# A linear-attention and expert block on Trainium2: keys with tokens on partitions made from the features' operands, behind the features' quad

## The chip, the cores and the metric

The kernel runs on one core of a Trainium2 chip. The core has a matrix engine (TensorE, PE in the profile, with its weight loads listed apart as PEld), a vector engine (VectorE, DVE), an activation engine (ScalarE, ACT), a general engine (GpSimd, POOL) and a queue that here only issues DMA transfers (SyncE, SP). Each works through its own list of instructions, and they are tied together by semaphores. Matrix products land in PSUM, which has eight banks of 128 partitions by 512 float32 values; everything else lives in SBUF. The metric is the time of one execution on the device in microseconds (us), lower is better, taken as the median of several runs.

## The reference

Input x is 2 x 2048 x 256, float32. Two residual steps follow each other, each scaled and shifted by a small modulation (`ca, sa, ga` and `cb, sb, gb`, computed from `L0_c` and `L0_wmod`):

```python
def _phi(x, omega):                       # 16 heads of 16; omega is 16 x 128
    proj = jnp.einsum('bhtd,dm->bhtm', x, omega)
    norm_sq_half = 0.5 * jnp.sum(x * x, axis=-1, keepdims=True)
    return jnp.exp(proj - norm_sq_half) / math.sqrt(m)
...
kv = phi_k[..., :, None] * v[..., None, :]
S = jnp.cumsum(kv, axis=2)                # running sum over tokens
Z = jnp.cumsum(phi_k, axis=2)
num = jnp.einsum('bhtm,bhtmd->bhtd', phi_q, S)
den = jnp.einsum('bhtm,bhtm->bht', phi_q, Z)[..., None] + EPS
y = num / den                             # then @ W_proj + b_proj
```

The second step is a feed-forward net (256 to 1024 to 256, relu) with four experts that differ by low-rank additions of rank 4; a router picks two of the four for each token and weighs their outputs:

```python
base = jnp.einsum('bsd,fd->bsf', x, Wi)
lora = jnp.einsum('bser,efr->bsef', jnp.einsum('bsd,erd->bser', x, A), B)
h = jax.nn.relu(base[:, :, None, :] + lora)
out = jnp.einsum('bse,bsed->bsd', w, jnp.einsum('bsef,df->bsed', h, Wo))
```

## The kernel before

**Tiling.** The 4096 tokens are eight blocks of 512 (`N = 8`; blocks 0 to 3 are one sequence, 4 to 7 the other). Within a block the 16 heads are four groups of four, and the 512 tokens are four chunks of 128. The main loop (L1091) takes a block in eight rounds, `k = 0..7`: round k finishes two chunks of group k // 2, and prepares the next two, which the code calls `following`. A round is written (block, round) below.

**Attention in a round.** The running sum is handled chunk by chunk. `features` (L470) makes the exponents of 128 features for four heads, 512 tokens each: four products of 32 rows that lie side by side in the array, "the features' quad", each filling one bank; `exponentials` (L482) turns them into `phi` on ACT. Features are on partitions and tokens along the row there. `scores` (L545) multiplies key features by query features within a chunk into the two fixed banks `pa[0]` and `pa[1]`; `mask` (L559) multiplies that by a triangle on DVE; `outputs` (L609) adds the masked scores times v and the earlier state times the query features into a bank `py`; `keep_outputs` (L632) copies it out on ACT. The state needs the keys the other way round, with tokens on partitions: `increments` (L569) multiplies such keys by v into the second half of the same bank `py`, `keep_increments` (L583) copies that out on DVE as `ds`, and in the next round `states` (L592) transposes and adds it to the state S.

**Two ways to have keys with tokens on partitions.** `keys` (L494) transposes `phi` chunk by chunk on PE into a bank `pk`, four transposes a chunk, and `keep_keys` (L539) copies the bank on ACT; `turn` (L1098) does this for both chunks of `following`. `key_rows` (L515) instead multiplies the features' operand f by omega with the roles exchanged, 32 rows and 128 columns a head, and `keep_key_rows` (L527) applies the exponential on ACT. Before, this second way is used only where a unit of the feed-forward net has four open banks with unused second halves.

**The rest of the work.** While attention of block i runs, the other work is laid between its parts by `run_full` (L946), whose table `steps` says for each round what PE does before scores: for the next block (`a = i + 1`) the transposes `channels1`, the products `query_key` and `values`; for the block before (`p = i - 1`) `project`, `channels2`, `low_rank`, `weigh`; and for `p` or `q = i - 2` the feed-forward net. Its first half goes in units: `hidden` (L826) opens four banks, `first` (L842) and `second` (L852) add the two experts' low-rank parts and apply relu, on ACT and on DVE (`r`, L864); `finish` (L867) is its second half. `unit_keys` (L970) is a unit whose banks also take key rows. In blocks 2 to 6 rounds 0, 1, 2 and 7 hold a unit, and their keys come from it; rounds 3 to 6 hold none. Blocks 0 and 1 have no unit but the one in (1, 7), and it takes no keys.

**Banks.** PSUM is shared by three kinds of tile: `pa[0]` and `pa[1]`, one bank each; "mm" tiles (`mm_tile`, L84), a ring of four banks; and "side" tiles (`side_tile`, L87), a ring of two. A ring hands out its banks in turn, and a new tile waits until its bank has been read. The features' quad takes all four "mm" banks, `py` takes a "side" bank.

**Order.** The order of instructions on each engine is the order in which the code writes them; `keep_written_order` (L22) fixes it. After `run_full` a round writes what `whole` (L1054) lists for it (layer norm statistics and norms on DVE, gates), the router in round 5, then scores, increments and outputs, the two copies, the quad for a later group with its exponentials, the masks, what `amid` (L1035) lists (the division, and the SP transfers that bring the operands f of the next block from DRAM, `reload`, L444), and `behind` (L1070: loads, the choice of experts, the bias).

Of the kernel before, what the change touches and what calls it, by code (L numbers as in the profile page):

```python
# [14 lines left out]
P = 128  # L15
NH = 16
DH = 16
# [15 lines left out]
def kernel(  # L33
# [53 lines left out]
    def side_tile(name):  # L87
        return psum.tile([P, TB], FP, tag="side", name=name, bufs=2)
# [291 lines left out]
    def query_key(i, n):  # L380
        s = st[i]
        pq = side_tile(f"pq{i}_{n}")
# [67 lines left out]
    def values(i, t):  # L450
# [4 lines left out]
        pv = side_tile(f"pv{i}_{t}")  # L455
# [59 lines left out]
    def key_rows(chunks, banks):  # L515


        for j, bank in enumerate(banks):
            rs = slice(2 * DH * j, 2 * DH * (j + 1))
            for i, g, t in chunks:  # L520
                c0 = TH + (t % 2) * P
                nc.tensor.matmul(  # L522
                    bank[:, c0 : c0 + P], st[i]["feat"][1, g][rs, t * P : (t + 1) * P], om[rs, :],
                    start=False, stop=True, skip_group_check=True, tile_position=(2 * DH * j, 0),
                )

    def keep_key_rows(chunks, banks):  # L527
        kts = [key_tile(*chunk) for chunk in chunks]
        i, g, t = chunks[0]
        n = len(chunks)  # L530
        for j, bank in enumerate(banks):
            nc.scalar.activation(
                pair[i, g, t // 2][:, 0:n, j, :],
                bank[:, TH : TH + n * P].rearrange("p (n m) -> p n m", m=M), AF.Exp, bias=lnm,
            )
        for chunk, kt in zip(chunks, kts):
            turned[chunk] = kt

    def keep_keys(i, g, t):  # L539
        if (i, g, t) in turned:  # L540
# [311 lines left out]
    def second(i, u, chunks=()):  # L852

        s = st[i]
        banks, f0, ts, whole_banks = s["unit"].pop(u)
        if chunks:
            key_rows(chunks, whole_banks)
        low_step(s, 1, banks, f0, ts)
        if chunks:
            keep_key_rows(chunks, whole_banks)  # L860
        for j, ph in enumerate(banks):
            g = s["g"][f0 + j][:, ts]
            r = work.tile([P, TH], FP, tag="r", name=f"r{i}_{u}{j}", bufs=RG)
            nc.vector.scalar_tensor_tensor(r, ph, 0.0, s["rho"][:, ts], ALU.max, ALU.mult)  # L864
            nc.gpsimd.tensor_add(g, g, r)  # L865
# [77 lines left out]

    PAIRS = NG * NT // 2

    def run_full(i, k, turn, state, following):  # L946


        a, p, q = i + 1, i - 1, i - 2

        def qk(n):
            query_key(a, n)

        def v(*ts):
            for t in ts:
                values(a, t)

        def ff(t, *part):
            finish(q, t, *part)
            if t == 3 and (not part or part[-1] == NF):  # L960
                store(q)

# [7 lines left out]
        def unit_keys(of, which, *between):  # L970
# [3 lines left out]
                do(*args)  # L974
            second(of, which, [chunk for chunk in following if carried(chunk[0], chunk[2])])

        def projection():
            project(p, 0, NT)

        mm, side, s = (turn, mm_tile), (turn, side_tile), (state,)  # L980
        split = (turn, side_tile, (0,)), (turn, mm_tile, (1,))
        if i == 0:
            steps = (
                (s, (values, 0, 2), (values, 0, 3), mm),
                (s, *split),
                (s, (channels1, a, side_tile, mm_tile), mm, (qk, 2)),
                (s, (qk, 0), mm),
                (s, (qk, 3), (gate, 0, 0), mm),
                (s, (v, 0), (gate, 1, 0), mm),
                (s, (v, 1, 2), (columns, 1), mm),  # L990
                (s, (qk, 1), (v, 3), mm),
            )
        elif i == 1:
            steps = (
                (s, (channels1, a, side_tile, mm_tile), mm, (qk, 2), (v, 0), (gate, 0, 1)),
                (s, (qk, 0), (v, 1), mm),
                (s, mm, (projection,)),
                (s, (qk, 3), mm),
                (s, *split, (channels2, p), (gate, 1, 1)),
                (s, *split),  # L1000
                (s, *split),
                (s, (v, 2), (low_rank, p), (qk, 1), (weigh, p), side, (hidden, p, 0),
                 (unit, p, 0, (v, 3))),
            )
        elif a < N:
            steps = (
                ((channels1, a), (hidden, q, 1), s, (v, 0), (unit_keys, q, 1, (qk, 2))),
                (s, (v, 1), (hidden, q, 2), (unit_keys, q, 2, (qk, 0))),
                (s, (v, 2), (hidden, q, 3), (unit_keys, q, 3, (qk, 3))),
                (s, (projection,), mm),  # L1010
                (s, (ff, 0), (channels2, p), mm),
                (s, (ff, 1), mm),
                (s, (ff, 2), mm, (low_rank, p)),
                ((weigh, p, side_tile), (state, mm_tile), (ff, 3, mm_tile, 0, NF), (v, 3),
                 (hidden, p, 0), (unit_keys, p, 0, (qk, 1))),
            )
        else:
            half = side_tile, 0, RG
            rest = None, RG, NF
            steps = (  # L1020
                (s, (turn, side_tile, (0,)), (hidden, q, 1),
                 (unit, q, 1, (turn, side_tile, (1,)))),
                (s, (ff, 0, *half), (hidden, q, 2), (unit, q, 2, (ff, 0, *rest), side)),
                (s, (ff, 1, *half), (hidden, q, 3), (unit, q, 3, (ff, 1, *rest), side)),
                (s, (projection,), mm),
                (s, *split, (channels2, p)),
                (s, *split),
                ((ff, 2), s, mm),
                ((low_rank, p), (ff, 3, side_tile, 0, 3), (weigh, p), s, (ff, 3, None, 3, 6),
                 (hidden, p, 0), (unit, p, 0, (ff, 3, None, 6, NF))),  # L1030
            )
        for do, *args in steps[k]:
            do(*args)

    def amid(i, k):  # L1035
# [8 lines left out]
                norm2(p)  # L1044
        if a < N:
            late = int(i == 0)
            n = {2 + late: 2, 3 + late: 0, 4 + late: 3, 7: 1}.get(k)
            if n is not None:
                reload(a, n, 0)
                reload(a, n, 1)  # L1050
# [6 lines left out]
        (0, 6): ((norm1_stats, 2),),  # L1057
        (0, 7): ((norm1, 2),),
        (1, 1): ((gate_wo, 0, 0, NF),),
        (1, 3): ((norm2, 0), (norm1_half, 3, 0)),  # L1060
        (1, 4): ((norm1_half, 3, 1),),
        (1, 5): ((gate_wo, 1, 0, NF),),
        (1, 6): ((choose, 0),),
        (1, 7): ((norm1, 3),),
    }
    for i in range(2, N - 2):
        whole[i, 4] = ((norm1_stats, i + 2),)
        whole[i, 6] = ((norm1, i + 2),)

    def behind(i, k):  # L1070
# [20 lines left out]
    for i in range(N):  # L1091
        for k in range(PAIRS):
# [146 lines left out]
```

## Time and profile before

| | us |
|---|---|
| median of 3 runs | 758.35 (757.79 to 758.4) |
| the profiled execution | 756.79 |
| its span, first to last instruction | 755.0 |
| PE busy / weight loads busy | 744.8 / 552.1 |
| DVE / ACT / POOL busy | 407.0 / 329.6 / 148.3 |
| granted TensorE clock | 1.00 |

The profile is of one execution. A row of the groups names the line, the engine and the operation, then the tile written and the tiles read ("out<-in"), the shape, the number of instructions, then the busy time in us, the mean length of one in ns, and after the second bar the time for which the engine stood idle just before them, with what ended it. Matrix products of float32 appear twice each, as do their weight loads. The view in order of time lists the start in us, the length, the engine, the line and the tiles, with equal neighbours merged; a bracket at the end gives the idle time just before and what released it. Products overlap in the array, so lengths of PE rows overlap too; the distance from one group's start to the next one's is what a group takes.

### The profile page before, as it was taken

To read this page: it belongs to the slowest core of one execution; us is meant where nothing else is said; L and a number is where in the kernel's file an instruction comes from. 1 tells how busy PE (TensorE), PEld (TensorE's weight loads), DVE (VectorE), ACT (ScalarE), POOL (GpSimd) and SP (SyncE) were. 2 spreads that over 40 slices of the span, in tenths; PEclk is the share of its full clock that TensorE was granted. 3 is DMA by queue.
4 is the path that set the end of the run, shared out by engine and by line. 5 is a ranking of instruction groups with operands and counts; after the bars stand their busy time and mean duration, and the time that the engine had idled before them with its cause. 6 is when DMAs were issued, how large, how long until landed. Compare 5 with 4: busy or idle time off the path is not lost.

```text
span 755.0 us, 24542 instructions
## 1 busy us (share of the span) xinstructions
PE 744.8 (99%) x10720; PEld 552.1 (73%) x10720; DVE 407.0 (54%) x1133; ACT 329.6 (44%) x742; POOL 148.3 (20%) x192
## 2 busy tenths in 40 slices
PE   9999999999999999999999999999999999999998
PEld 6667776666787767776787677877688777777776
DVE  5667667564663547534656456645364424654612
ACT  1665546535544444435544455435454343521010
POOL 3000322222210322011220122103130112005122
PEclk9999999999999999999999999999999999999999
DMA  4369443123301433023420342204240130002000
GB/s 134 111 195 298 146 143 100 44 82 120 114 29 32 129 112 114 17 72 119 124 72 33 111 125 82 67 29 130 73 127 16 50 110 17 16 34 83 1 29 28
DMA packets 44234, 65.46 MB, mean 87 GB/s; under 512 B 6752, under 2 KB 20256, under 8 KB 44128
## 3 DMA queue, kind: packets, MB, share of 16 engines
q1 hardware_dynamic: 42240, 62.33, 26.1%
q8 instruction: 84, 1.38, 0.8%
q10 hardware_dynamic: 1888, 1.58, 0.7%
q14 instruction: 22, 0.18, 0.1%
HBM read 35.32 MB, written 28.57 MB: 85 GB/s over the span
## 4 chain that ended last, share of the span: by engine, by line
PE 93%; DVE 4%; ACT 1%; issue 1%; DMA 0%; POOL 0%; DVEq 0%
PE ph L836 13%; PE pf L874 12%; PE pa L552 9%; PE pp L476 9%; PE pq L384 7%; PE ph L821 4%; PE pk L500 4%; PE pv L457 4%; PE py L621 4%; PE py L576 4%; PE py L627 3%; PE po L682 3%; PE pt L597 3%; PE pf L896 2%; PE ph L522 2%; PE pta L331 1%
## 5 line engine op out<-in xcount | busy, mean ns | idle before, releaser
L865 POOL TENSOR_TENSOR g<-g,r 128x256 f32<-128x256 f32 x128 | 90.6, 741 | 416.3 <-DVE r L864 416.3
L487 ACT ACTIVATE phi<-pp,lnm 128x512 f32<-128x512 f32 x256 | 155.2, 689 | 9.7 <-PE pp L476 3.6
L874 PE MATMUL pf<-wo_g,g 128*128 128x256 f32 x448 | 103.6, 382 | 0.4 <-ACT phi L487 0.2
L836 PE MATMUL ph<-h,wi_sb 128*128 128x256 f32 x448 | 101.9, 380 | 0.1
L836 PEld LDWEIGHTS ph<-h,wi_sb 128*128 128x128 f32 x448 | 84.3, 190 | 12.5 <-DVE r L864 0.5
L874 PEld LDWEIGHTS pf<-wo_g,g 128*128 128x128 f32 x448 | 82.6, 190 | 13.7 <-issue 2.2
L552 PEld LDWEIGHTS pa<-phi,phi 128*32 128x32 f32 x4096 | 77.5, 110 | 14.8 <-issue 13.3
L552 PE MATMUL pa<-phi,phi 128*32 128x128 f32 (+3 forms) x4096 | 85.4, 235 | 0.1
L850 ACT ACTIVATE g<-ph 128x256 f32<-128x256 f32 x112 | 33.9, 389 | 115.1 <-PE ph L821 115.1
L635 ACT COPY y<-py 128x128 f32<-128x128 f32 x128 | 27.8, 269 | 125.2 <-DVE ds L588 123.4
L561 DVE TENSOR_TENSOR am<-pa,causal 128x512 f32<-128x512 f32 x128 | 81.8, 681 | 0.0
L391 DVE TENSOR_SCALAR qs<-pq,bqk 128x512 f32<-128x512 f32 x30 | 22.5, 751 | 99.3 <-PE pq L384 94.6
L476 PE MATMUL pp<-f,om 32*128 32x512 f32 x512 | 73.6, 640 | 0.0
L542 ACT COPY kt<-pk 128x512 f32<-128x512 f32 x82 | 44.5, 594 | 54.8 <-PE pk L500 54.7
L864 DVE SCALAR_TENSOR_TENSOR r<-ph,rho 128x256 f32<-128x256 f32 x112 | 41.7, 422 | 45.6 <-PE ph L821 23.2
L384 PE MATMUL pq<-hT,w_sb 128*128 128x512 f32 x120 | 58.5, 612 | 0.0
L588 DVE COPY ds<-py 128x256 f32<-128x256 f32 (+1 forms) x63 | 25.7, 407 | 52.6 <-PE py L627 47.0
L621 PE MATMUL py<-am,v 128*32 128x128 f32 x1024 | 51.4, 273 | 0.0
L627 PE MATMUL py<-phi,S 128*32 128x128 f32 x960 | 50.1, 273 | 0.0
L597 PEld LDWEIGHTS pt<-ident,ds 128*128 128x128 f32 x120 | 12.8, 140 | 44.6 <-DVE ds L588 38.7
L500 PE MATMUL pk<-ident,phi 128*128 128x128 f32 x328 | 44.9, 275 | 0.5 <-ACT phi L487 0.4
L500 PEld LDWEIGHTS pk<-ident,phi 128*128 128x128 f32 x328 | 37.7, 141 | 7.1 <-ACT phi L487 3.0
(159 smaller groups left out, 968.2 us busy)
## 6 DMA issues: line engine op xcount, KB each, us to landing
f<-qd SPq DMA_DIRECT2D x60, 256.0 KB
qd<-qs SPq DMA_DIRECT2D x58, 256.0 KB
ydr<-y SPq DMA_DIRECT2D x32, 256.0 KB
num<-ydr SPq DMA_DIRECT2D x16, 256.0 KB
inv<-rdr SPq DMA_DIRECT2D x16, 256.0 KB
xt<-in_x_dram SPq DMA_DIRECT2D x7, 512.0 KB
out_dram<-xt SPq DMA_DIRECT2D x7, 512.0 KB
wo_g<-in_woT_dram SPq DMA_DIRECT2D x2, 1024.0 KB
```

Source lines behind the costliest of these rows:

```text
L384: nc.tensor.matmul(pq, w_sb[:, k, n * P : (n + 1) * P], s["hT"][:, k, :], start=(k == 0), stop=(k == KC - 1),)
L476: nc.tensor.matmul(pp, om[rs, :], f[rs, :], start=True, stop=True, tile_position=(2 * DH * j, 0))
L487: nc.scalar.activation(ph, pps[j], AF.Exp, bias=lnm)
L500: nc.tensor.transpose(pk[:, j * P : (j + 1) * P], phi[i, g, 1, j][:, t * P : (t + 1) * P], ident)
L542: nc.scalar.copy(kt.rearrange("p h m -> p (h m)"), turned[i, g, t])
L552: nc.tensor.matmul(pa[t % 2][c * CG : (c + 1) * CG, j * P + q0 : j * P + q1], phi[i, g, 1, j][:, t0 + c * CG : t0 + (c + 1) * CG], phi[i, ...
L561: nc.vector.tensor_mul(am, pa[t % 2][:].rearrange("p (h q) -> p h q", h=HG), causal[t % 2][:].unsqueeze(1).to_broadcast([P, HG, P]),)
L621: nc.tensor.matmul(py[rows[j], :], v[:, t, g * HG + j, :], am[:, j, :], start=True, stop=state is None,)
L627: nc.tensor.matmul(py[rows[j], :], state[:, rows[j]], phi[i, g, 0, j][:, tok], start=False, stop=True,)
L836: nc.tensor.matmul(ph, wi_sb[:, k, f * P : (f + 1) * P], s["h2"][:, k, ts], start=(k == 0), stop=False, skip_group_check=True,)
L865: nc.gpsimd.tensor_add(g, g, r)
L874: nc.tensor.matmul(po, s["g"][f][:, t * P : (t + 1) * P], wo_g[i // NBLK][:, f, :], start=(f == 0), stop=(f == NF - 1), skip_group_check=True,
```

## The change

The rounds without a unit get their keys from `key_rows` too. A new function `keys_behind_features` takes four banks, `pa[0]`, `pa[1]` and two "side" tiles, writes the key rows of `following` there at the very start of the round, which is straight behind the quad that ended the round before, and has ACT apply the exponential to them. `key_rows` and `keep_key_rows` get the first column and the start flag as arguments. Which round does what is told by two new functions:

```diff
+    def keys_behind_features(i, g, t):
+        banks = pa + [side_tile(f"pk{i}_{g}{t}{n}") for n in range(2)]
+        chunks = [(i, g, u) for u in (t, t + 1) if carried(i, u)]
+        key_rows(chunks, banks, 0, True)
+        keep_key_rows(chunks, banks, 0)
...
+    def keys_first(i, k):
+        return i == 0 or (k < 7 if i == 1 else 3 <= k <= 6 if i < N - 1 else 3 <= k <= 5)
+
+    def keys_in_unit(i, k):
+        return k == 7 if i == 1 else 1 < i and (k < 3 or k == 7) and (i < N - 1 or k in (1, 2))
...
+        tile = mm_tile if keys_first(i, k) else side_tile
...
+        if keys_first(i, k):
+            keys_behind_features(*following[0])
         for do, *args in steps[k]:
             do(*args)
```

In those rounds the state step, `query_key`, `values`, `project`, `finish` and block 0's and 1's `channels1` take "mm" tiles in place of "side" tiles, and `mm`, `side` and `split`, the turns, leave the table of steps. Two rows of it, as examples:

```diff
-                (s, (projection,), mm),
-                (s, (ff, 0), (channels2, p), mm),
+                (s, (projection,)),
+                (s, (ff, 0), (channels2, p)),
```

Rounds (1, 7), (7, 1) and (7, 2) change from a unit and turns to `unit_keys`; (1, 7) also gets a new order of its steps (`low_rank` first, the values `v` and `query_key` later), and values 1 move from (1, 1) to (1, 2). Turns stay in (7, 0) and (7, 6) and for the first two chunks of all.

The order at the end of a round changes in every round, and outputs come ahead of increments wherever keys come from `key_rows`:

```diff
-            late_keys = 1 < i < N - 1 and k in (0, 1, 2, 7)
+            late_keys = keys_first(i, k) or keys_in_unit(i, k)
             if late_keys:
                 outputs(i, g, (t, t + 1), bank)
             added = increments(following, bank)
             if not late_keys:
                 outputs(i, g, (t, t + 1), bank)
+            for chunk in following:
+                mask(*chunk)
             keep_increments(*added)
             keep_outputs(i, g, (t, t + 1), bank)
 
             gi, gg = divmod(n // NT + 1 + k % 2, NG)
             if gi < N:
                 exponentials(*features(gi, gg, k % 2))
-            for chunk in following:
-                mask(*chunk)
```

Some smaller steps move to other rounds:

```diff
-            n = {2 + late: 2, 3 + late: 0, 4 + late: 3, 7: 1}.get(k)
+            n = {2 + late: 2, 3 + late: 0, 6: 3, 7: 1}.get(k)
...
-        (1, 3): ((norm2, 0), (norm1_half, 3, 0)),
-        (1, 4): ((norm1_half, 3, 1),),
-        (1, 5): ((gate_wo, 1, 0, NF),),
+        (1, 2): ((norm1_half, 3, 0),),
+        (1, 3): ((norm2, 0),),
+        (1, 5): ((norm1_half, 3, 1), (gate_wo, 1, 0, NF)),
...
     for i in range(2, N - 2):
-        whole[i, 4] = ((norm1_stats, i + 2),)
         whole[i, 6] = ((norm1, i + 2),)
```

The statistics taken out of round 4 are now a step of round 2 (`next_stats`, between `values` and `hidden`); the loads of the key operands f of groups 2 and 3 go from round 4 (5 in block 0) to round 6.

More of the change, by code (lines that the diff above doesn't have):

```diff
@@ L378, in channels1, with query_key @@
         s["feat"], s["qd"] = {}, {}
-    def query_key(i, n):
+    def query_key(i, n, tile=side_tile):
         s = st[i]
-        pq = side_tile(f"pq{i}_{n}")
+        pq = tile(f"pq{i}_{n}")
         for k in range(KC):
@@ L448, in reload, with values @@
         st[i]["feat"][side, g] = f
-    def values(i, t):
+    def values(i, t, tile=side_tile):
         s = st[i]
@@ L454, in values @@
             nc.gpsimd.memset(s["v"][:, :, :, DH:HW], 1.0)
-        pv = side_tile(f"pv{i}_{t}")
+        pv = tile(f"pv{i}_{t}")
         for k in range(KC):
@@ L513, in key_tile, with key_rows @@
         return pair[n][:, t % 2]
-    def key_rows(chunks, banks):
+    def key_rows(chunks, banks, c0, start):
         for j, bank in enumerate(banks):
@@ L520, in key_rows, with keep_key_rows @@
             for i, g, t in chunks:
-                c0 = TH + (t % 2) * P
+                c = c0 + (t % 2) * P
                 nc.tensor.matmul(
-                    bank[:, c0 : c0 + P], st[i]["feat"][1, g][rs, t * P : (t + 1) * P], om[rs, :],
-                    start=False, stop=True, skip_group_check=True, tile_position=(2 * DH * j, 0),
+                    bank[:, c : c + P], st[i]["feat"][1, g][rs, t * P : (t + 1) * P], om[rs, :],
+                    start=start, stop=True, skip_group_check=True, tile_position=(2 * DH * j, 0),
                 )
-    def keep_key_rows(chunks, banks):
+    def keep_key_rows(chunks, banks, c0):
         kts = [key_tile(*chunk) for chunk in chunks]
@@ L533, in keep_key_rows @@
                 pair[i, g, t // 2][:, 0:n, j, :],
-                bank[:, TH : TH + n * P].rearrange("p (n m) -> p n m", m=M), AF.Exp, bias=lnm,
+                bank[:, c0 : c0 + n * P].rearrange("p (n m) -> p n m", m=M), AF.Exp, bias=lnm,
             )
@@ L856, in second @@
         if chunks:
-            key_rows(chunks, whole_banks)
+            key_rows(chunks, whole_banks, TH, False)
         low_step(s, 1, banks, f0, ts)
         if chunks:
-            keep_key_rows(chunks, whole_banks)
+            keep_key_rows(chunks, whole_banks, TH)
         for j, ph in enumerate(banks):
@@ L944 @@
     PAIRS = NG * NT // 2
+    def keys_first(i, k):
+        return i == 0 or (k < 7 if i == 1 else 3 <= k <= 6 if i < N - 1 else 3 <= k <= 5)
+    def keys_in_unit(i, k):
+        return k == 7 if i == 1 else 1 < i and (k < 3 or k == 7) and (i < N - 1 or k in (1, 2))
     def run_full(i, k, turn, state, following):
         a, p, q = i + 1, i - 1, i - 2
+        tile = mm_tile if keys_first(i, k) else side_tile
         def qk(n):
-            query_key(a, n)
+            query_key(a, n, tile)
         def v(*ts):
             for t in ts:
-                values(a, t)
+                values(a, t, tile)
         def ff(t, *part):
-            finish(q, t, *part)
+            finish(q, t, *(part or (tile,)))
             if t == 3 and (not part or part[-1] == NF):
@@ L975, in unit_keys, with next_stats @@
             second(of, which, [chunk for chunk in following if carried(chunk[0], chunk[2])])
+        def next_stats():
+            if i + 2 < N:
+                norm1_stats(i + 2)
         def projection():
-            project(p, 0, NT)
-        mm, side, s = (turn, mm_tile), (turn, side_tile), (state,)
-        split = (turn, side_tile, (0,)), (turn, mm_tile, (1,))
+            project(p, 0, NT, tile)
+        mm, side, s = (turn, mm_tile), (turn, side_tile), (state, tile)
         if i == 0:
             steps = (
[L984 to L991, printed above, removed]
+                (s, (values, 0, 2, tile), (values, 0, 3, tile)),
+                (s,),
+                (s, (channels1, a, tile, tile), (qk, 2)),
+                (s, (qk, 0)),
+                (s, (qk, 3), (gate, 0, 0)),
+                (s, (v, 0), (gate, 1, 0)),
+                (s, (v, 1, 2), (columns, 1)),
+                (s, (qk, 1), (v, 3)),
             )
@@ L994, in run_full @@
             steps = (
[L995 to L1003, printed above, removed]
+                (s, (channels1, a, tile, tile), (qk, 2), (v, 0), (gate, 0, 1)),
+                (s, (qk, 0)),
+                (s, (v, 1), (projection,)),
+                (s, (qk, 3)),
+                (s, (channels2, p), (gate, 1, 1)),
+                (s,),
+                (s,),
+                ((low_rank, p), s, (v, 2), (weigh, p), (v, 3), (hidden, p, 0),
+                 (unit_keys, p, 0, (qk, 1))),
             )
@@ L1008, in run_full @@
                 (s, (v, 1), (hidden, q, 2), (unit_keys, q, 2, (qk, 0))),
-                (s, (v, 2), (hidden, q, 3), (unit_keys, q, 3, (qk, 3))),
-                (s, (projection,), mm),
-                (s, (ff, 0), (channels2, p), mm),
-                (s, (ff, 1), mm),
-                (s, (ff, 2), mm, (low_rank, p)),
+                (s, (v, 2), (next_stats,), (hidden, q, 3), (unit_keys, q, 3, (qk, 3))),
+                (s, (projection,)),
+                (s, (ff, 0), (channels2, p)),
+                (s, (ff, 1)),
+                (s, (ff, 2), (low_rank, p)),
                 ((weigh, p, side_tile), (state, mm_tile), (ff, 3, mm_tile, 0, NF), (v, 3),
@@ L1022, in run_full @@
                  (unit, q, 1, (turn, side_tile, (1,)))),
[L1023 to L1027, printed above, removed]
+                (s, (ff, 0, *half), (hidden, q, 2), (unit_keys, q, 2, (ff, 0, *rest))),
+                (s, (ff, 1, *half), (hidden, q, 3), (unit_keys, q, 3, (ff, 1, *rest))),
+                (s, (projection,)),
+                (s, (channels2, p)),
+                (s,),
                 ((ff, 2), s, mm),
```

## The prediction

> **What bounds the kernel now.** I read the engine shares first, then the groups of instructions kept apart by shape, then the order of time at the seams between rounds, and last the waits. A round is named (block, round); f is the start of a features quad, and times "at +x" are from f.
>
> ```profile
> PE 744.8 (99%) x10720; PEld 552.1 (73%) x10720; DVE 407.0 (54%) x1133; ACT 329.6 (44%) x742; POOL 148.3 (20%) x192
> ...
> L500 PE MATMUL pk<-ident,phi 128*128 128x128 f32 x328 | 44.9, 275 | 0.5 <-ACT phi L487 0.4
> L542 ACT COPY kt<-pk 128x512 f32<-128x512 f32 x82 | 44.5, 594 | 54.8 <-PE pk L500 54.7
> L532 ACT ACTIVATE kt<-ph,lnm 128x256 f32<-128x256 f32 x72 | 28.0, 471 | 0.0
> L522 PE MATMUL ph<-om,f 32*128 32x128 f32 x304 | 14.4, 297 | 0.0
> ```
>
> PE is the bound everywhere: it waits almost nowhere, so its time is the sum of its groups, and I take a group's price from its start to the next group's start. In the order of time a turn of two chunks (eight transposes, L500) holds PE for 0.97 us, key rows of two chunks (L522) for 0.55, of one 0.33; a state step 0.28, scores 1.14, increments and outputs 1.44, a features quad 1.07. ACT, 44% busy, looks free on average, but the question is what it has in front of it at one moment. A seam without a unit, (1,3) into (1,4):
>
> ```profile
> 120.24 1.14 PE L476 MATMUL pp<-f,om 32*128 32x512 f32 x8
> 120.38 0.42 DVE L588 COPY ds<-py 128x256 f32<-128x256 f32 x1 [0.67 <-PE py L627]
> 120.72 1.28 DVE L561 TENSOR_TENSOR am<-pa,causal 128x512 f32<-128x512 f32 x2
> 120.84 0.43 ACT L635 COPY y<-py 128x128 f32<-128x128 f32 x2 [1.88 <-DVE ds L588]
> ...
> 121.40 2.42 ACT L487 ACTIVATE phi<-pp,lnm 128x512 f32<-128x512 f32 x4
> ...
> 122.14 0.42 PEld L500 LDWEIGHTS pk<-ident,phi 128*128 128x128 f32 x4 [0.19 <-ACT phi L487]
> ...
> 122.72 0.42 PEld L331 LDWEIGHTS ptf<-ident,xhf 128*128 128x128 f32 x4 [0.16 <-ACT phi L487]
> ```
>
> The quad fills all four "mm" banks, and these come free only as ACT's exponentials drain them: at +1.90 (122.14), +2.48 (122.72), +3.06, +3.64. The exponentials hang on a chain: the DVE copy ds, then ACT's y copies, then phi. The state step at +1.07 escapes the chain because it uses a "side" bank.
>
> A seam behind a unit, (2,0) into (2,1), f = 181.71:
>
> ```profile
> 180.01 1.52 DVE L864 SCALAR_TENSOR_TENSOR r<-ph,rho 128x256 f32<-128x256 f32 x4 [1.13 <-ACT kt L532]
> 181.84 0.42 DVE L588 COPY ds<-py 128x256 f32<-128x256 f32 x1 [0.31 <-PE py L576]
> 182.19 1.28 DVE L561 TENSOR_TENSOR am<-pa,causal 128x512 f32<-128x512 f32 x2
> ```
>
> The r's end at -0.18, held by ACT's key exponentials on the same banks. Here ds starts at +0.13 and the 1.28 us of masks come after it, where nobody waits for them.
>
> **The change, part by part.**
>
> *Turns become key rows.* 38 rounds (block 0: eight, block 1: seven, blocks 2 to 6: rounds 3 to 6, block 7: rounds 3 to 5) exchange 0.97 for 0.55. The Trainium skill ("TensorEngine Tiling (Array Packing)", Key Properties) adds that changing the tiling mode drains the array; the trace has it as 0.96 instead of 1.07 for the one quad per block that a product of the same tiling follows. By the rule the place straight behind the quad is worth another 38 x 0.11 = 4.2 us on top of 38 x 0.42 = 16; by the banks above it is worth nothing, since PE then meets a wait. I take the banks. The new forms have near rows: key rows between 0.44 (nothing but streaming) and 0.97, taken 0.55; four exponentials of 128x256 1.55 in all.
>
> *State and products move to "mm".* Features 0.96 and key rows 0.55 end at +1.5; state must wait to +1.90 and ends at +2.18; the next product waits for the second bank, +2.48. Scores came at 1.07 + 0.28 + X + 0.97 = 2.32 + X, X being the round's other PE work, and now come at 2.48 + X plus 0.1 at the change of tiling: the saving is used up, about +0.2 where X is long. Bounds: -0.4 if no bank is waited for, +0.7 if key rows also end late; (1,2) shows the very wait, its turn starting at +1.90. That is taken.
>
> *Key exponentials stand in front of scores.* They lie in pa, so scores (L552) cannot start before they are read. ACT takes them behind the fourth phi (which starts at +2.89): first bank free at +3.94, second at +4.30, so scores start at +4.25 in effect. Where X is under 1.7 (rounds with no or one short product) PE waits. The skill's same page (PSUM Bottleneck) says that tiling speeds TensorE but not the emptying of PSUM: here 2 copies of 0.594 become 1.55 us, and at the worst place of ACT's queue. Behind them queue only squares (L394), whose loads come rounds later.
>
> *Masks ahead of copies.* DVE takes its queue in order. With D the end of DVE's last work before the masks, ds starts at D + 1.1 if that is after +0.14, the y copies 0.46 later, the exponentials just before these end. Behind a unit D = -0.18: ds 1.37 at its end instead of 0.56, y copies 1.84 instead of 1.03, the four banks +0.57. The nearest row is a seam that is late already, (1,7) into (2,0), f = 155.20:
>
> ```profile
> 157.20 0.41 DVE L588 COPY ds<-py 128x256 f32<-128x256 f32 x1
> 157.65 0.43 ACT L635 COPY y<-py 128x128 f32<-128x128 f32 x2 [5.70 <-DVE ds L588]
> ...
> 158.13 0.66 PE L331 MATMUL pta<-ident,xha 128*128 128x128 f32 x4 [0.47 <-ACT y L635]
> ...
> 158.72 1.13 PE L836 MATMUL ph<-h,wi_sb 128*128 128x256 f32 x4
> ```
>
> There ds is 1.86 late, PE stands for the y copies and then for the banks, and hidden starts at +3.52 instead of +2.00: 1.5 lost, so about 0.4 of a lateness is free and the rest is paid. That r waits for kt, and y for ds, is what the Trainium skill ("PSUM — Partial Sum Buffer", PSUM bank collisions raise a hardware error) would have: two engines are kept off one bank, reads against reads too. It speaks against this change: were such reads free to overlap, r would end a microsecond earlier and this part would cost nothing; by the rows (22.1 us of that wait in 20 rounds) it stays.
>
> *Moves costed at nothing.* Block statistics of norm 1 (2.4 us DVE, 1.0 POOL) go into round 2, where DVE idles over 5 us ahead of qs; without that cover up to 2.4 a block. The two loads of features f move from round 4 to 6 on SP; the quad that reads them comes a block later; late, they would stop PE for their own transfer. POOL's add of the bias and SP's stores keep their places.
>
> **The sum**, in us:
> - A, behind units. Round 0 of blocks 3 to 6: hidden at +2.39 for 2.00, 0.4 each, 1.6; (2,0) 0.75. Rounds 1 and 2 of blocks 2 to 6: state at 1.43, v waits for y to 1.90, hidden at 2.77 for 2.22: 0.55 x 10 = 5.5. Round 3: the last key rows wait for y (1.90), state 2.47, first projection 3.05, scores 6.8 for 6.0: 0.8 x 5 = 4.0. Block 7, rounds 0, 2, 3: 0.5 + 0.5 + 0.8 = 1.8. Together 13.7 (9 to 18).
> - B, rounds 4, 5, 6 of blocks 2 to 6: 0.25 + 0.2, and 0.5 in round 6, where the router's small DVE steps (D = -0.45) now precede masks: 0.95 x 5 = 4.7 (0 to 8).
> - C, blocks 0 and 1, where statistics, norms and gates stand ahead of masks and their cover, the 0.97 of turns, is gone. Example (0,1): D = +0.4, exponentials 1.14 late, X = 0, scores at 4.25 + 1.14 = 5.4 for 3.25 (in effect: they now wait for phi), 2.15. Example (1,3): statistics after the projection, D = +0.3, state 3.22, query product 1.72, scores 5.3 for 4.0, 1.3. Likewise block 0: 0.1, 2.15, 0.75 (hT no longer behind a turn), 0.25, 0.25, 1.45, 1.05, 1.4 = 7.4; block 1: 1.3, -0.6, 0.5, 1.3, 0.3, 1.3, 1.6, 1.4 = 7.1. Together 14.5 (6 to 20).
> - D, (7,4) and (7,5): 0.4 + 1.3 = 1.7; turns that become unit keys in (7,1), (7,2): -0.9.
>
> Sum +33.7. The profiled execution took 756.79 (span 755.0 and 1.8 around it): 790.5; the median of the runs is 1.6 above that, 758.35, giving 792. I take **790**.
>
> **Rivals.** *Slower, but little (760 to 777).* DVE's or ACT's work fits earlier than I place it and C shrinks to a third, A to a half: 758 + 5 + 7 + 5 = 775. For it: late rounds give DVE more time; against: (2,0) shows lateness paid nearly in full.
> *Faster (742 to 757).* One mechanism at one place: the first free bank behind the quad. Were state and first product served by a bank not held by the quad, and the y copies early, key rows would be paid openly and the turns' price returned: -0.42 x 38 = -16, 742. It decides when state starts by +1.6 and scores are not held; a bank at +1.90 speaks against it in every round, and A must not eat it.
> *Nothing (within 0.2%).* Gain and waits cancel, as 16 saved and 14 of A lost would if B and C were nothing.
>
> **Numbers.** 0.70 for my case (own range 777 to 806), 0.15 slower by little, 0.12 faster, 0.03 the same. 0.2%, 1.5 us, is about what runs of this kernel can tell. The range, 763 to 806, leaves out the faster cases and some of the ends. The forecast is of the likeliest.
>
> **What will show it.** In the changed profile: key rows under pa and pk at about +1.0; state at +1.9 in keys-first rounds, not +1.07; in (0,1), (1,5), (1,6), (7,5) PE idle until ACT's kt, scores at +4.3 or later; ds behind units at +0.95, and hidden in (2..6,1) at +2.8; L500 down to 16 records, PE's busy share below 96%. I am wrong if state starts before +1.6, or if masks end by +0.1 behind units.

## The result and the profile after

The changed kernel takes **803.01 us** (median of 4 runs, 801.32 to 803.82) against 758.2 for the kernel before in runs beside it: a ratio of 1.0589, 95% interval 1.057 to 1.0607, slower by 45 us. Its profiled execution took 803.29 with a span of 801.6 (755.0 before). The forecast was 790, with a range of 763 to 806.

The page of the changed kernel, engine shares and the chain of work that ended last:

```profile
PE 772.9 (96%) x11032; PEld 571.2 (71%) x11032; DVE 420.7 (52%) x1133; ACT 343.2 (43%) x828; POOL 148.4 (19%) x192
...
PE 71%; DVE 16%; ACT 9%; issue 4%; DMA 0%; POOL 0%; DVEq 0%; ACTq 0%
```

The chain was 93% PE, 4% DVE and 1% ACT before. Now a quarter of it runs over DVE and ACT, which PE waits for. (Do not read the longer busy time of PE, 772.9 for 744.8, as more work: ends of products are modelled, and part of it ran at a lower clock, as shown below.) The groups, shapes kept apart:

```profile
L532 ACT ACTIVATE kt<-pk,lnm 128x256 f32<-128x256 f32 x70 | 31.0, 524 | 0.0
L532 ACT ACTIVATE kt<-pa,lnm 128x256 f32<-128x256 f32 x70 | 30.4, 508 | 0.0
...
L522 PE MATMUL pa<-om,f 32*128 32x128 f32 x292 | 30.3, 284 | 0.1
L522 PEld LDWEIGHTS ph<-om,f 32*128 32x128 f32 x344 | 12.1, 185 | 16.6 <-ACT g L857 15.9 <-issue 0.7
...
L500 PE MATMUL pk<-ident,phi 128*128 128x128 f32 x16 | 2.3, 276 | 0.0
```

The change does what it says: 16 records of turns are left of 328, and key rows lie in pa and pk. The seam behind a unit, (2,1) into (2,2), in order of time, f = 205.23:

```profile
203.54 1.52 DVE L872 SCALAR_TENSOR_TENSOR r<-ph,rho 128x256 f32<-128x256 f32 x4 [1.13 <-ACT kt L532]
204.98 1.28 DVE L568 TENSOR_TENSOR am<-pa,causal 128x512 f32<-128x512 f32 x2
205.23 1.14 PE L476 MATMUL pp<-f,om 32*128 32x512 f32 x8
206.17 0.41 DVE L595 COPY ds<-py 128x256 f32<-128x256 f32 x1
206.62 0.43 ACT L642 COPY y<-py 128x128 f32<-128x128 f32 x2 [2.09 <-DVE ds L595]
206.64 0.44 PE L604 MATMUL pt<-ident,ds 128*128 128x128 f32 x2 [0.27 <-DVE ds L595]
206.94 1.28 ACT L487 ACTIVATE phi<-pp,lnm 128x512 f32<-128x512 f32 x2
208.07 0.81 PE L843 MATMUL ph<-h,wi_sb 128*128 128x256 f32 x3
```

The masks now stand between r and ds, and what hangs on ds is late one after the other: ds starts at +0.94 (+0.13 before), phi at +1.71 (+1.16), the state step at +1.41 (+1.07), hidden at +2.84 (+2.2). The prediction worked with 1.43 and 2.77. (It calls this seam (2,0) into (2,1); by the count of rounds it is (2,1) into (2,2). No sum depends on the name.)

A keys-first round with nothing to lay over the wait, (1,5), f = 141.60:

```profile
141.60 1.14 PE L476 MATMUL pp<-f,om 32*128 32x512 f32 x8
142.76 2.42 ACT L487 ACTIVATE phi<-pp,lnm 128x512 f32<-128x512 f32 x4
143.50 0.44 PE L604 MATMUL pt<-ident,ds 128*128 128x128 f32 x2
144.08 0.38 PEld L716 LDWEIGHTS pr<-h,wga_sb 128*32 128x32 f32 x16 [0.38 <-ACT phi L487]
145.06 0.86 ACT L532 ACTIVATE kt<-pa,lnm 128x256 f32<-128x256 f32 x2
145.60 1.55 PE L559 MATMUL pa<-phi,phi 128*32 128x128 f32 x63 [0.88 <-ACT kt L532]
```

The state step starts at +1.90, the next product at +2.48, both when phi sets an "mm" bank free; scores start at +4.00 and stop once more for the second bank, because ACT empties the quad before the keys. The prediction had 1.90, 2.48 and 4.25 in effect.

By blocks, as the distance between features quads (f to f, in the order of time), us before, and what the changed kernel adds:

| block | 0 | 1 | 2 | 3 | 4 | 5 | 6 | 7, to (7,4) | rest |
|---|---|---|---|---|---|---|---|---|---|
| before | 56.87 | 68.29 | 91.20 | 88.00 | 88.92 | 89.57 | 89.78 | 51.12 | 131.3 |
| after | +11.28 | +7.25 | +7.06 | +4.45 | +4.54 | +4.25 | +3.73 | +2.60 | +1.4 |

The rest is the start, before the first round, and the end; 0.75 of its 1.4 lie in the start, which varies by as much from run to run (-0.3 to +1.3 in the runs below).

### The profile page after: what moved, and what is told of

It is laid out like the page before. It is cut to its first block, busy times and chain, and to the rows that moved or that the text cites. A ratio compares the mean times of both kernels' runs of the same rounds, so it can differ in the third digit from the quotient of the medians.

```text
span 801.6 us, 25301 instructions
## 1 busy us (share of the span) xinstructions
PE 772.9 (96%) x11032; PEld 571.2 (71%) x11032; DVE 420.7 (52%) x1133; ACT 343.2 (43%) x828; POOL 148.4 (19%) x192
## 3 DMA queue, kind: packets, MB, share of 16 engines
q8 instruction: 87, 1.43, 0.7%
## 4 chain that ended last, share of the span: by engine, by line
PE 71%; DVE 16%; ACT 9%; issue 4%; DMA 0%; POOL 0%; DVEq 0%; ACTq 0%
PE ph L843 13%; PE pf L882 12%; PE pq L384 7%; PE pa L559 6%; ACT phi L487 5%; DVE am L568 5%; PE pv L457 4%; DVE r L872 4%; PE pp L476 4%; PE po L689 3%; PE ph L828 3%; PE py L628 2%; DVE qs L391 2%; ACT kt L532 2%; PE py L634 2%
## 5 line engine op out<-in xcount | busy, mean ns | idle before, releaser
L843 PE MATMUL ph<-h,wi_sb 128*128 128x256 f32 x448 | 103.9, 386 | 0.1
L559 PEld LDWEIGHTS pa<-phi,phi 128*32 128x32 f32 x4096 | 78.6, 111 | 25.0 <-issue 13.7
L559 PE MATMUL pa<-phi,phi 128*32 128x96 f32 (+3 forms) x4096 | 88.5, 238 | 5.2 <-ACT kt L532 5.2
L614 DVE TENSOR_TENSOR S<-pt,S 128x128 f32<-128x128 f32 x112 | 32.1, 287 | 50.5 <-PE pt L604 48.6
L628 PE MATMUL py<-am,v 128*32 128x128 f32 x1024 | 54.3, 280 | 0.0
L634 PE MATMUL py<-phi,S 128*32 128x128 f32 x960 | 52.4, 280 | 0.0
L887 DVE TENSOR_TENSOR xt<-pf,xt 128x256 f32<-128x256 f32 x28 | 11.9, 424 | 66.1 <-PE pf L882 66.1
L522 PE MATMUL pk<-om,f 32*128 32x128 f32 x292 | 43.7, 295 | 1.0 <-DVE sc L755 0.2
L522 PEld LDWEIGHTS pa<-om,f 32*128 32x128 f32 x292 | 28.8, 185 | 19.7 <-issue 9.7
L583 PE MATMUL py<-kt,v 128*32 128x128 f32 x944 | 39.8, 276 | 0.0
```

The source lines that it names most:

```text
L522: nc.tensor.matmul(bank[:, c : c + P], st[i]["feat"][1, g][rs, t * P : (t + 1) * P], om[rs, :], start=start, stop=True, skip_group_check=T ...
L559: nc.tensor.matmul(pa[t % 2][c * CG : (c + 1) * CG, j * P + q0 : j * P + q1], phi[i, g, 1, j][:, t0 + c * CG : t0 + (c + 1) * CG], phi[i, ...
L628: nc.tensor.matmul(py[rows[j], :], v[:, t, g * HG + j, :], am[:, j, :], start=True, stop=state is None,)
L634: nc.tensor.matmul(py[rows[j], :], state[:, rows[j]], phi[i, g, 0, j][:, tok], start=False, stop=True,)
L843: nc.tensor.matmul(ph, wi_sb[:, k, f * P : (f + 1) * P], s["h2"][:, k, ts], start=(k == 0), stop=False, skip_group_check=True,)
```

## The experiments

Three theories stood: (1) masks ahead of copies delay ds, the y copies and the banks; (2) behind the quad PE waits for the ring of "mm" banks, so that key rows save nothing there; (3) in blocks 0 and 1 scores wait for ACT's key exponentials and for late DVE work. The rivals: the loss comes from the other half of each edit, from DVE being full, or from the clock.

**Masks ahead only where the next round needs pa.**

```diff
+            ni, nk = divmod(i * PAIRS + k + 1, PAIRS)
+            masks_now = ni < N and keys_first(ni, nk)
-            for chunk in following:
+            for chunk in following if masks_now else []:
                 mask(*chunk)
...
                 exponentials(*features(gi, gg, k % 2))
+            for chunk in following if not masks_now else []:
+                mask(*chunk)
```

> The changed kernel, with masks ahead of the copies only where the next round begins with key rows in pa; in all other rounds they stand behind the exponentials again. Theory (masks behind r delay ds, the y copies and the four banks behind every unit): in blocks 3 to 6 rounds 0, 1, 2 fall back by 0.49, 0.63 and 0.62 to 12.0 to 12.9 us, round 3 keeps its +0.7; with (2,0) and (7,0) some -11 to -14 us, so 789 to 792. Rival (what costs at these seams is the new order of the rest, not the masks): no change, 803.

Measured: 789.32 us, ratio 1.0418 (1.0363 to 1.0473). In blocks 3 to 6 rounds 0, 1 and 2 are back within 0.11 of their times before, but for (5,2) with +0.30 and (6,2) with -0.21; round 3 keeps +0.69 to +1.14; (7,0) is back to 10.59, while (2,0) returns only to 16.85 (why is told below). Theory 1 holds behind units.

**Masks ahead alone, in the kernel before.**

```diff
+            for chunk in following:
+                mask(*chunk)
             keep_increments(*added)
...
                 exponentials(*features(gi, gg, k % 2))
-            for chunk in following:
-                mask(*chunk)
```

> The kernel before with only one part of the change: masks ahead of the copies in all rounds. Theory: the seams behind units pay as in the changed kernel (0.5 to 0.6 in rounds 0, 1, 2 of blocks 2 to 6, some 9 us), rounds 3 and 6 of these blocks pay 0.2 to 0.5, blocks 0 and 1 up to 3: +12 to +18, 770 to 776. Rival (masks ahead cost only together with key rows in pa): 758 to 760.

Measured: 788.3, ratio 1.038 (1.0352 to 1.0408): +30, twice what I expected. Behind units it is as expected (0.48 to 0.74, but for (2,0) with 2.88, part of it at a lower clock). But rounds without a unit pay too, and not for a busy DVE: round 4 pays 0.39 to 0.40 and block 0 3.25, although DVE had time there. The waits of this run name it:

```profile
DVE am L561 <- PE py L621: 30.3, 25, 3.3
```

DVE stood 30.3 us in all ahead of masks, in 25 waits of up to 3.3, for `outputs`. The tile `am` has two buffers, one for each chunk; masks for the next pair cannot be written until this round's outputs have read the last pair. With the masks behind the copies that was always long past.

**A third buffer for `am`**, in that kernel and in the changed one (two small tiles of the choice of experts get one buffer instead of two, to make room):

```diff
-        am = work.tile([P, HG, P], FP, tag="am", name=f"am{i}_{g}{t}")
+        am = work.tile([P, HG, P], FP, tag="am", name=f"am{i}_{g}{t}", bufs=3)
```

> The kernel before with masks ahead of the copies in all rounds, as in that earlier run, and a third buffer for the masked scores am (and one buffer less for two small tiles of the choice of experts, to make room). Theory (with two buffers the masks of the next pair wait until this round's outputs have read the last pair, which puts them 0.3 to 0.4 later than scores would allow): the 0.4 that rounds without a unit pay for masks ahead goes, while rounds behind a unit, where r is the last to finish, keep theirs: -10 to -14 against that run, 774 to 778. Rival (it is DVE's own queue that is full): no change, 788.

Measured: 779.18, 9 us less. Its waits:

```profile
DVE am L561 <- PE pa L552: 15.0, 17, 2.6
DVE am L561 <- PE py L621: 0.4, 1, 0.4
```

The wait for outputs is gone; masks wait for scores, as they must. Round 4 of blocks 3 to 6 is at +0.00, block 0 at +1.19, and behind units the 0.49 to 0.74 stay, since r holds those. Round 5 of blocks 2 to 5 keeps +0.9 to +1.2. The view of DVE at the start of (2,5), f = 219.78, shows why:

```profile
219.06 0.39 DVE L297 BATCH_NORM_STATS2 statsa<-xt 128x6 f32<-128x256 f32 x1
219.49 0.18 DVE L298 BATCH_NORM_AGGREGATE mva<-statsa 128x2 f32<-128x6 f32 x1
219.71 0.17 DVE L302 TENSOR_SCALAR rstda<-mva 128x4 f32<-128x4 f32 x1
219.78 1.28 DVE L561 TENSOR_TENSOR am<-pa,causal 128x512 f32<-128x512 f32 x2
220.98 0.41 DVE L588 COPY ds<-py 128x256 f32<-128x256 f32 x1
```

The norm's statistics, which this kernel still has in round 4 of these blocks, hold the masks, and these hold ds (+1.20). Block 6 has no such statistics, and its round 5 stands at +0.00. The change had moved them to round 2.

> The changed kernel with the third buffer for am (same room made). Theory: masks start right behind scores, ds and the y copies come 0.2 earlier in keys-first rounds and the last key rows with them, but the state step still waits for the first mm bank at +1.9: little, 0 to -4, 799 to 803. Rival (am's buffers are the larger part of the loss in keys-first rounds): -8 or more.

Measured: 801.39, 1.6 less. In the changed kernel the buffer is a small part, and this run tells what holds the state step there: in (5,5) ds starts at +0.14 instead of +0.32 and the last key row at +1.52 instead of +1.69, but the state step still at +1.90. The first exponential ends at +1.85 in both: the bank decides, not masks or key rows.

**Masks behind the exponentials everywhere, in the changed kernel.**

> The changed kernel with masks behind the exponentials in all rounds, the other part alone. Theory: the seams behind units come back (-10 or more), late statistics no longer push the exponentials in blocks 0 and 1, but key rows in pa now wait for the masks until +1.8 and the state step starts at about +2.4 instead of +1.9, 0.2 to 0.3 in each of 38 rounds: 792 to 799. Rival (key rows cannot do without early masks): above 803.

Measured: 786.81, more than expected was saved. Blocks 3 to 6 stand at +1.65, +2.19, +2.17 and +1.97, no worse than with masks by need (+2.69, +2.58, +2.57, +1.97). So masks ahead of copies do not pay even where key rows go into pa: with late masks rounds 4, 5 and 6 of block 5 cost 0.60 each, against 0.42, 0.36 and 0.71 with masks by need, and round 3 costs 0.37 against 0.79. In this run (1,7) is 6.7 longer than before. PE stands 3.05 us in it, and from within that wait on the granted clock is half for 10.2 us; half of what PE works in that time, up to 4.6, can be the clock's.

**Blocks 0 and 1 as before.** All of their steps, turns and order, with the change kept from block 2 on.

> The changed kernel with blocks 0 and 1 wholly as in the kernel before (turns, order of steps, masks behind the exponentials). Theory: these two blocks return to their 56.9 and 68.3 us (-18.5) and (2,0) to 14.5 or less (-3.6), with them most of the windows of half clock: 780 to 782. Rival (part of the loss of blocks 0 and 1 comes from elsewhere, such as the clock or code loading): above 786.

Measured: 780.82, as the theory had it. The blocks are at -0.01 and +0.56, (2,0) at 14.50. So 18.0 us arose in these two blocks and 3.6 in the round behind them.

**The state step behind the first product**, in rounds 3 to 6 of blocks 2 to 6:

```diff
-                (s, (projection,)),
-                (s, (ff, 0), (channels2, p)),
+                ((projection,), s),
+                ((ff, 0), s, (channels2, p)),
```

(and likewise in rounds 5 and 6.)

> The changed kernel; in rounds 3 to 6 of blocks 2 to 6 the state step goes behind the first product, so that the product and not the state takes the first free mm bank. Theory (the product waits for the second bank of the ring, drained at +2.48): it starts at +1.9, 0.3 saved in each of 20 rounds, -6 us, 797. Rival (key rows or masks hold PE, not the ring): no change, 803.

Measured: 795.81, 7.2 less. Round (6,5) of the changed kernel, in order of time, f = 610.00:

```profile
610.00 0.31 PEld L476 LDWEIGHTS pp<-f,om 32*128 32x128 f32 x8 [0.20 <-DVE am L568]
...
611.90 0.20 PEld L604 LDWEIGHTS pt<-ident,ds 128*128 128x128 f32 x2
612.48 0.94 PEld L882 LDWEIGHTS pf<-wo_g,g 128*128 128x128 f32 x5 [0.38 <-ACT phi L487]
```

and of this run, f = 604.69:

```profile
604.69 0.31 PEld L476 LDWEIGHTS pp<-f,om 32*128 32x128 f32 x8 [0.20 <-issue]
...
606.59 1.59 PEld L882 LDWEIGHTS pf<-wo_g,g 128*128 128x128 f32 x8
```

Whichever comes first starts at +1.90. In the changed kernel the product comes second and waits to +2.48; here the state step is second, at +5.46 behind the product, and waits for nothing. Key rows and masks are as they were, so the 0.58 was the second bank of the ring (theory 2). Round 5 falls from +0.36 to 0.00, round 6 from +0.71 to +0.35. Of the 7.2 us some 6 are saved in blocks 2 to 6; 1.6 are a stretch of lower clock in (7,0) that this run's profile lacks.

**The clock: the changed kernel once more, and its waits filled.** In the changed kernel the granted clock was 0.989 on average, 1.000 in the profile before. The windows view, whose columns are the stretch, its length, the busy times of PE, PEld, DVE, ACT and POOL with their counts, then PEclk, the DMA share and GB/s, finds five stretches of 3.41 us at half the clock in the rounds, in (0,1), (0,5), (1,6), (2,0) and (7,0); I call them slow windows. That of (0,5) and the equal time ahead of it, and the whole round:

```profile
71.61:75.02 3.41, 3.23 (x24) 2.18 (x21) 1.75 (x5) 2.10 (x6) 0.00 (x0) 1.00 0.90 250
75.02:78.44 3.42, 3.42 (x25) 2.33 (x27) 0.97 (x3) 2.12 (x6) 0.00 (x0) 0.50 1.03 391
...
70.87:80.70 9.83, 9.65 (x151) 6.88 (x147) 5.59 (x15) 4.22 (x10) 0.00 (x0) 0.83 0.93 307
```

> The changed kernel once more, unchanged, for its granted clock. Theory (the clock falls to half for one window of 3.4 us after a window in which TensorE stood, and the windows do not start with the kernel): again a handful of such windows, some in other rounds than (0,1), (0,5), (1,6), (2,0), (7,0); a round that has one is about 1.6 us longer than the same round without one. Rival (these rounds are long by their own waits): the same lengths, wherever the windows fall.

Measured: 803.83, a single run. The same round of the same program, second execution:

```profile
70.87:79.06 8.19, 8.02 (x150) 5.88 (x150) 5.34 (x14) 4.22 (x10) 0.00 (x0) 1.00 0.92 311
```

One execution has half the clock for 3.41 of 9.83 us (mean 0.83) and takes 9.83; the other has the full clock and takes 8.2. In this second execution the slow windows lie in (0,1), (2,0) and (7,0) again, but not in (0,5) and (1,6); one lies in (1,7), behind a long wait. There the two executions, the first one ahead:

```profile
157.55 1.14 PE L476 MATMUL pp<-f,om 32*128 32x512 f32 x8
160.27 1.24 PE L800 MATMUL pl<-ident,los 128*128 128x128 f32 x8 [1.57 <-ACT phi L487]
...
154.42 1.14 PE L476 MATMUL pp<-f,om 32*128 32x512 f32 x8
158.77 1.24 PE L800 MATMUL pl<-ident,los 128*128 128x128 f32 x8 [3.21 <-ACT phi L487]
```

(1,6) takes 8.88 with a slow window and 7.23 without, but nothing is gained: the first product of (1,7) starts 11.6 us after the f of (1,6) in both (148.68 and 147.19), because DVE works off the choice of experts, then masks and ds, at its own pace (`los` ends some 8.95 after that f in both), and the wait is 1.64 longer where PE came earlier. So the slow window of (1,6) costs nothing in the end, while that of (1,7), behind the wait, is worth 1.6: the round takes 20.20 instead of 16.93, half of it by the longer wait.

What sets a slow window off is only partly shown. In the 3.41 us ahead of the five of the first execution PE is busy for 1.80, 3.23, 1.79, 1.75 and 2.90 us. Ahead of (0,1), (1,6) and (2,0) PE stands in one wait of 1.6 to 1.7; ahead of (0,5) and (7,0), no wait is longer than 0.6. In those two, narrow products, key rows of 32 rows and low-rank products of 16, start one by one as their banks come free, and the profile counts PE as busy. And (7,0) is no place of the change alone: a later run, whose (7,0) is that of the kernel before, has a slow window there too. The profiled execution of the kernel before has none in its rounds, but others of its executions were granted down to 0.993 of the clock, where in them is not on record.

For the filled waits the key rows of the first bank are issued again and thrown away, six times in (0,1), five in (0,5) and (1,6), as are the first channel transposes in (2,0):

```diff
+        for _ in range(again):
+            key_rows(chunks, banks[0:1], 0, True)
         key_rows(chunks, banks, 0, True)
```

> The changed kernel; the waits at the start of (0,1), (0,5), (1,6) and (2,0) are filled with products that are thrown away: the key rows of the first bank five or six times more, the first channel transposes of (2,0) four times more. Theory (idle TensorE costs its clock for the next 3.4 us window): the windows of half clock leave these rounds and each is about 1.6 us shorter, though it has more work: -5 to -7, 796 to 798. Rival (the clock is not what lengthens them): no gain, 803 to 806.

Measured: 801.6, only 1.4 less: a miss as a remedy. (2,0) falls to 16.62 from 18.12 and (1,6) to 7.28 from 8.88, with the full clock in both; but (0,1) keeps its slow window, the filling itself lengthens (0,5) to 8.82, against 8.20 without either, and a slow window comes up in (1,7), 19.68. The one in (1,7) was there without filling too, when (1,6) had none; so this run does not show that filling moves a window, only that it was no remedy.

**Key rows where banks are free, in the kernel before.** If the waits and not the key rows are at fault, key rows should pay in the place of the turn: just ahead of scores, where all four "mm" banks are empty.

```diff
+        def rows_ahead():
+            chunks = [chunk for chunk in following if carried(chunk[0], chunk[2])]
+            banks = [mm_tile(f"pk{i}_{k}{n}") for n in range(HG)]
+            key_rows(chunks, banks, 0, True)
+            keep_key_rows(chunks, banks, 0)
...
-                (s, (projection,), mm),
-                (s, (ff, 0), (channels2, p), mm),
-                (s, (ff, 1), mm),
-                (s, (ff, 2), mm, (low_rank, p)),
+                (s, (projection,), rows),
+                (s, (ff, 0), (channels2, p, side_tile), rows),
+                (s, (ff, 1), rows),
+                (s, (ff, 2), (low_rank, p, side_tile), rows),
```

> The kernel before; in rounds 3 to 6 of blocks 2 to 6 and in (7,3) the turn becomes key rows just ahead of scores, in the four mm banks, which are free by then; channels2 and low_rank take side banks; outputs ahead of increments; masks stay behind. Theory (key rows pay when no bank is waited for): 0.97 becomes 0.55, -0.42 less small waits in 21 rounds, -7 to -9: 749 to 751. Rival (emptying four banks by ACT holds the next quad): 757 or slower.

Measured: 762.65, ratio 1.0059 (1.0043 to 1.0076): slower by a little. In blocks 2, 4, 5 and 6 rounds 3 and 5 gain 0.20 each, not 0.42; round 4 gains nothing (+0.10), and round 6 loses 1.19 (block 3: -0.20, +0.30, -0.48, +0.76). In round 6 `low_rank`, now in a "side" bank, waits for the S additions, which DVE does behind the choice of experts; in (5,6):

```profile
495.59 1.09 PE L793 MATMUL pl<-ident,los 128*128 128x128 f32 x8 [1.16 <-DVE S L607]
```

Why 0.20: with products tiled otherwise on both sides key rows take longer than beside products tiled like themselves, as the start of the next group shows:

```profile
477.41 0.75 PE L522 MATMUL pk<-om,f 32*128 32x128 f32 x16
478.09 1.33 PE L552 MATMUL pa<-phi,phi 128*32 128x128 f32 x64
```

0.68 us, against 0.55 inside a unit; and in (5,3) and (5,5) they start 0.1 later than the turn did. That the change of tiling is the cause fits these rows; no run separates it.

The next run keeps only the places that gained, and takes the units of (1,7), (7,1) and (7,2), as well as (0,7), (1,1), (1,2) and (7,3):

> The kernel before, with key rows only where nothing waits for their banks and no small step is displaced: just ahead of scores in the mm banks in rounds 3 and 5 of blocks 2 to 6, in (0,7), (1,1), (1,2) and (7,3), and in the open units of (1,7), (7,1), (7,2). Masks stay behind. The rows-in-mm run showed 0.20 saved in rounds 3 and 5 (key rows 0.68 there, not 0.55, since the array changes its tiling on both sides), the changed kernel 0.7 and 0.2 in (7,1) and (7,2), and (1,2) now loses its wait for the first bank. Theory: -2.0 - 0.2 - 0.9 - 0.3 - 1.1 = -4.5, 753 to 756. Rival (the emptying on ACT delays increments or quads): 758 or slower.

Measured: 757.29, ratio 0.9988 (0.9972 to 1.0004): not to be told from the kernel before. Rounds 3 and 5 give 0.20 each again and (7,1) 0.71. But (1,2) loses 0.39; (1,7) and (7,0) are 2.2 and 1.6 longer with slow windows in them, of which (2,0) gives 1.5 back; and round 6 of blocks 2, 4 and 5 loses 0.51, 0.76 and 0.14, while that of block 3 gains 0.30. (2,6), f = 221.77, shows where:

```profile
230.43 0.27 PE L621 MATMUL py<-am,v 128*32 128x128 f32 x1
230.93 0.31 PE L621 MATMUL py<-am,v 128*32 128x128 f32 x4 [0.22 <-issue]
```

Up to here every group of the round starts where it did before (these outputs at +8.66 for +8.65). Then PE stops for half a microsecond in the middle of its outputs, and the profile names no engine that it waits for. Why it stops there, and in block 3 did so in the kernel before, stays open.

The last run has (1,2) as before and mends (1,7); against the kernel before:

```diff
-                (s, (v, 2), (low_rank, p), (qk, 1), (weigh, p), side, (hidden, p, 0),
-                 (unit, p, 0, (v, 3))),
+                (s, (v, 2), (low_rank, p), (weigh, p), (v, 3), (hidden, p, 0),
+                 (unit_keys, p, 0, (qk, 1))),
```

> The rows-where-free kernel, mended where its rounds were longer than before: (1,2) as before; in (1,7) the query product goes between the two halves of the unit, where the earlier order left TensorE idle. Key rows stay in rounds 3 and 5 of blocks 2 to 6, in (0,7), (1,1), (7,3) and in the units of (1,7), (7,1), (7,2). Theory: -0.2 x 13 and -0.9 in block 7, up to -1.4 over (1,7) and (2,0), and no window of half clock in (1,7): -3 to -5, 753 to 755. Rival (what is saved in these rounds comes back as waits in rounds 6 or 7, or as a window of half clock elsewhere): 757 to 759.

Measured: 757.54, ratio 0.9989 (0.9977 to 1.0000). Its profiled execution, with the full clock, has a span of 753.1 for 755.0; block 7 is 1.12 shorter and blocks 3 to 6 1.3 in all, while (1,7) and (2,0) are 0.3 and 0.9 longer: there the rival was right. In (2,0) it is r again, which ends at -0.25 for -1.34, since the unit of (1,7) now has keys and r waits for them. No version here beats the kernel before by more than runs can tell.

## Why the prediction was right, and where its sum was short

The direction was right, so were the main waits, and 803 lies in the range, three below its end. The sum, +33.7, falls 13 short of the span's +46.6. By its own terms, from the distances between quads:

| term | predicted | measured |
|---|---|---|
| A, behind units | 13.7 | 19.3 |
| B, rounds 4 to 6 of blocks 2 to 6 | 4.7 | 7.7 |
| C, blocks 0 and 1 | 14.5 | 18.5 |
| D, (7,4) and behind it | 1.7 | 0.9 |
| units in (7,1), (7,2) | -0.9 | -0.9 |
| start, and round 7 of blocks 2 to 6 | 0 | 1.0 |

(In (7,2) units and masks come together, +0.24; the split takes -0.2 for the unit, as in the last two runs.)

**A.** Sized well: 0.49 for 0.4 in round 0, 0.62 in most for 0.55 in rounds 1 and 2, 0.70 in most for 0.8 in round 3, and, but for round 3, undone by moving the masks back. The short part is two rounds: (2,0), 3.6 for 0.75, and (7,0), 2.1 for 0.5. (7,0) is a slow window: 11.07 instead of 12.68 in three runs without one. In (2,0) hidden starts at +5.46 for +3.52, and then takes 5.24 for 3.56, which is the slow window, 1.7. The 1.9 ahead of it are two things: r ends 1.1 later because (1,7) became a unit with keys (worth 0.9 in the last run, which has that without the masks), and the masks. The prediction took the end of r from (1,7) before, where the unit had no keys.

**B.** The term was too small: 0.2 for a state step and a product that each wait for a bank, against 0.36 to 0.42, and 0.71 for 0.5 in round 6. The prediction also had ds at +0.14 in these rounds; it looked for DVE's last work and not for what the masks write, and in (5,5) `am`'s two buffers put ds at +0.32. That cost next to nothing here: with the third buffer these rounds stand at 7.5 instead of 7.7.

**C.** Of the 3.8 of (0,1) 1.5 is a slow window (half of the 3.05 us of it that lie in the round); the other 2.3 were worked out as 2.15. Another slow window, in (0,5), is worth 1.6. Together they are most of the 3.9 by which block 0 is over. Block 1 measured 7.25 for 7.1, in part by luck: rounds 0 to 5 were 0.9 below, (1,6) and (1,7) 1.1 above, where DVE's choice of experts set the pace.

**The clock** is what the prediction lacked altogether: it took the granted clock of 1.00 over. The slow windows of (0,1), (0,5), (2,0) and (7,0), at 1.6 to 1.7 each, are some 6.5 of the 13 us, an estimate from these rounds; that of (1,6) was hidden in the wait behind it. With the clock of the kernel before the sum would have been about 6.5 short, of which 3.0 are B and 1.2 the rest of (2,0).

**The signs.** State came at +1.90 at the earliest, ds behind units at +0.94, hidden at +2.84, 16 records of turns were left. Two did not come: PE's busy share came to 96.4%, not below 96%, and scores of (1,5) came at +4.00, before +4.3.

**The key rows' price** of 0.55 came from a place where the neighbour is tiled alike. Behind the quad it did not matter, as the bank decided. The rule on changes of tiling, which I put at 0.11 a change and then set aside, would explain why the gain is halved wherever key rows stand alone: 0.20 for 0.42.

**Rivals.** *Faster* fell at the point it named: in none of the 38 keys-first rounds did state start before +1.90, and where ds is late it starts later (+3.26 in (0,1)). *Slower, but little* needed C at a third and A at a half; even without their slow windows they are about 15 and 16. *Nothing* would have needed B and C to vanish.

## What to carry to other kernels

An instruction that is moved up in an in-order queue brings its own waits with it: look at the buffers it writes and at what else must come out of that queue next, not only at when its inputs are ready. When the busiest engine is made faster, ask which bank its next product takes and when that bank is emptied; what is saved ahead of that moment brings nothing, and the same held for a slow clock ahead of a wait. A kernel that opens waits on TensorE can lose clock behind them as well: here some 6.5 us, which a sum of waits does not have.

## What the runs showed of the hardware

The clock was not expected. In the profiled execution of the changed kernel five stretches of 3.41 us had half the granted clock, worth about 1.6 us each where no wait followed, in rounds that differ between two executions of one program. Their starts (44.30, 75.02, 153.53, 180.84 and 655.29) lie 9, 23, 8 and 139 times 3.413 us apart: one even grid, whatever the rounds do. The Trainium skill ("TensorE: Matmul & The Clock Gate", The HAM clock gate) describes it: activity is watched in free-running windows of 3.4 us, and an idle one halves the clock. Length, grid and change of place agree. How idle a window must be these runs don't show. It need not be idle throughout: the slow windows followed 3.41 us in which the profile has PE busy for 1.75 to 3.23.
